# Layer 0 of a four-layer convolution stack: depthwise taps as one product per 4x4 patch, joined with pixels on partitions

## The chip, the cores and the metric

The kernel runs on one core of a Trainium2 chip. A core has five engines with a queue of their own each: TensorE (matrix products, with a separate row for its weight loads in the profile, PE and PEld), VectorE (DVE), ScalarE (ACT), GpSimd (POOL) and SyncE (SP, used for issuing transfers). Products land in PSUM, eight banks of 2 KB per partition; everything else lives in SBUF (128 partitions) or in device memory. The metric is the device time of one execution in microseconds, as the median of three runs: 3287.07 us (3285.98 to 3290.96).

## The reference

The input is x, 8 images of 128 channels and 56x56 pixels, float32. Four residual layers follow each other, `x = x + layer(norm(x))`. The change touches only the first:

```python
# 7x7 windows of 8x8 pixels; 8 heads of 16 channels; 4 windows chosen per window
xw = windows of groupnorm(x)
q, k, v = split(xw @ W_qkv + b_qkv)
v_img = v put back into an image
lepe = depthwise 3x3 convolution of v_img (padding 1) + lepe_b
r_idx = top 4 of mean(q) * SCALE . mean(k) over windows
attn = softmax(q * SCALE . k of the four windows)     # per head, 64 x 256
o = attn @ (v of the four windows)
x = x + (o + lepe) @ W_o + b_o
```

Layer 1 is a recurrent layer along the pixels, layer 2 a grouped 3x3 convolution with a 1x1 part, layer 3 two 3x3 convolutions with batch norm.

## The kernel before

**Layout.** X holds all images with channels on partitions. A strip is 7 windows, 8 rows of pixels, 448 columns (`BLK`); an image has 7 strips, the layer 56. Windows are worked on in pairs: 196 pairs, 3.5 to a strip. `xw` holds the normalised image window by window.

**A pair.** `gather` (GpSimd) copies the keys of the four chosen windows into `ks` (line 498, eight copies for a pair) and makes `qm`, the queries of the window twice, once masked to the even and once to the odd heads (line 500). `scores` makes their products on four row groups at once (539). `maxima` takes row maxima on VectorE (546), four ops; `halve` splits them in two bfloat16 parts on GpSimd (552, 553), `flip` transposes these on TensorE (558), `flipped` copies them on ScalarE (562). `shifted` makes the transposed scores less the maxima (571, 581), `exponentials` runs on ScalarE (591). `values` multiplies with the chosen windows' values (605), which `fetch` brings from `vpix` in device memory into `ring` (518). `turned` transposes 32x32 blocks on VectorE so that pixels lie on partitions (617), `divide` takes the reciprocal of the sums and the quotients `ot` (626, 629), and then transposes `ot` back to channels on partitions (638) into a strip's tile `o`.

**A strip's jobs.** `normalise` (278, VectorE; three of the first image's strips on ScalarE, 276) and `sums` (283); keys (291), image (301, with `image_end` 307 into `vrow`, stored to `vimg`, the value image with a border, by `store` 202 or 204), pixels (319, stored to `vpix`), queries (390, 394). `neighbours` (407) loads three copies of a strip's rows with their upper and lower rows from `vimg`, shifted by a column each, 32 channels at a time, from GpSimd's queue. `depthwise` (420) makes the taps: for each of three rows and four channel groups a product with 96 rows (3 shifts x 32 channels) and 448 columns, summed in PSUM over the three rows; ScalarE adds the bias (427). `join` adds `o` to it (438, GpSimd; the last one on VectorE). `project` multiplies with W_o (446) and adds to X in one VectorE op (451); the result is kept in `xkeep` (452) and measured for layer 1 (460).

**Order.** The order on TensorE, ScalarE, VectorE and GpSimd is written out by hand. Step p runs the list `SHORT` or `LONGER` of acts: scores and maxima of pair p + 2, shifted scores and exponentials of p + 1, values, turn and division of p, gathers for p + 3. A planner puts jobs with a ready and a due time into two places of each step, `one` and `two`, and small ones into `light`; the taps are `LONG` and take `two`. VectorE work such as normalisations and statistics is hooked behind the acts of a step by weights. `ahead` issues the transfers collected in `later` from GpSimd. Each act has its PSUM bank: values share a bank with the first quarter of the scores, `one` and `two` share banks with the shifted scores, swapped in `LONGER`.

Of the kernel before, what the change touches and what calls it, by code (L numbers as in the profile page):

```python
# [20 lines left out]
P = 128  # L21
# [13 lines left out]
PW = HW + 2  # L35
EPS = 1e-5
# [10 lines left out]
def conv_stack_kernel(ctx: ExitStack, tc: tile.TileContext, a: dict, out: bass.AP):  # L47
# [81 lines left out]
    with ExitStack() as l0:  # L129
# [18 lines left out]
        wlep = load("wlep", [3 * CL, 3, 4, CL], a["lepe_d"], nc.sync)  # L148
# [4 lines left out]
        lbv = c0.tile([P, 1], F32, name="lbv")  # L153
        ones = c0.tile([P, P], BF16, name="ones")
# [13 lines left out]
        vimg = [dram.tile([P, PW, PW], F32, name=f"vimg{i}", tag=f"vimg{i}") for i in range(2)]  # L168
        vpix = [dram.tile([NWIN + 1, WPX, P], F32, name=f"vpix{i}", tag=f"vpix{i}") for i in range(B)]
        vrow = []  # L170
        for i in range(2):
            t = c0.tile([P, WS, PW], F32, name=f"vrow{i}", tag=f"vrow{i}")
            if i == 0:
                nc.gpsimd.memset(t, 0.0)
                for k in range(2):
                    nc.sync.dma_start(vimg[k][:, 0:PW:PW - 1, :], t[:, 0:2, :])
            else:
                nc.gpsimd.memset(t[:, :, 0:PW:PW - 1], 0.0)
            vrow.append(t)
# [3 lines left out]
        qs, ks, selrs, v3s, lepes, os_, st1, norms = {}, {}, {}, {}, {}, {}, {}, {}  # L183
# [77 lines left out]
        def preparation(b):  # L261
# [9 lines left out]
            def normalise(i, scalar=False):  # L271

                dst = xw[:, i * NW : (i + 1) * NW, :].rearrange("p j (u v) -> p j u v", v=WS)
                src = X[:, b, i * BLK : (i + 1) * BLK].rearrange("p (u j v) -> p j u v", u=WS, v=WS)
                if scalar:
                    nc.scalar.activation(dst, src, AF.Identity, bias=st["off"], scale=st["r"])
                else:
                    nc.vector.tensor_scalar(dst, src, st["gm"], st["r"], ALU.subtract, ALU.mult)
# [20 lines left out]
            def image_mm(i):  # L299
                st["pv", i] = psum([P, BLK], f"pvt_{b}_{i}")  # L300
                nc.tensor.matmul(  # L301
                    st["pv", i], wqkv[:, 2 * P :], xwf[:, i * BLK : (i + 1) * BLK], start=True, stop=True
                )

            def image_end(i):
                t = vrow[(b * NBLK + i) % 2]
                nc.scalar.activation(
                    t[:, :, 1 : 1 + HW].rearrange("p u (j v) -> p j u v", v=WS),
                    st["pv", i].rearrange("p (j u v) -> p j u v", u=WS, v=WS),
                    AF.Identity, bias=bqkv[:, 2:3],  # L310
                )
                store(begun, nc.sync, vimg[b % 2][:, 1 + i * WS : 1 + (i + 1) * WS, :], t)
# [72 lines left out]
        def queries(b, i):  # L385
            st = {}

            def mm():
                st["pq"] = psum([P, BLK], f"pq_{b}_{i}")
                nc.tensor.matmul(st["pq"], wqkv[:, :P], xwf[:, i * BLK : (i + 1) * BLK], start=True, stop=True)  # L390

            def end():
                q = strip.tile([P, NW, WPX], F32, name=f"q_{b}_{i}", tag="q", bufs=2)
                nc.scalar.activation(
                    q.rearrange("p j x -> p (j x)"), st["pq"], AF.Identity, bias=bqs, scale=QSCALE
                )
                qs[b, i] = q

            return fill(mm, end)

        def neighbours(b, i):

            t = strip.tile([3 * CL, 4, (WS + 2) * PW], F32, name=f"v3_{b}_{i}", tag="v3", bufs=1)
            flat = vimg[b % 2].rearrange("(g c) u v -> c g (u v)", c=CL)
            for k in range(3):
                n = (WS + 2) * PW - k
                nc.gpsimd.dma_start(
                    t[k * CL : (k + 1) * CL, :, :n], flat[:, :, i * WS * PW + k : i * WS * PW + k + n]
                )
            v3s[b, i] = t  # L410

        def depthwise(b, i):
            st = {}

            def mm():
                rows = v3s.pop((b, i)).rearrange("p g (u v) -> p g u v", v=PW)
                st["pl"] = psum([P, WS, HW], f"plep_{b}_{i}")
                for dy in range(3):
                    for g in range(4):
                        nc.tensor.matmul(  # L420
                            st["pl"][g * CL : (g + 1) * CL], wlep[:, dy, g, :], rows[:, g, dy : dy + WS, :HW],
                            start=(dy == 0), stop=(dy == 2),
                        )

            def end():
                lepes[b, i] = strip.tile([P, WS, HW], F32, name=f"lep_{b}_{i}", tag="lep")
                nc.scalar.activation(lepes[b, i], st["pl"], AF.Identity, bias=lbv)
# [5 lines left out]
        def join(b, i):  # L433

            o, t = os_.pop((b, i)), lepes[b, i]
            engine = nc.vector if (b, i) == (B - 1, NBLK - 1) else nc.gpsimd
            t = t.rearrange("p u (j v) -> p u j v", v=WS)
            engine.tensor_add(t, t, o.rearrange("p j (u v) -> p u j v", v=WS))

        def project(b, i):  # L440
# [3 lines left out]
            def mm():  # L444
                st["py"] = psum([P, BLK], f"py_{b}_{i}")
                nc.tensor.matmul(  # L446
# [1501 lines left out]
```

## Time and profile before

| | |
|---|---|
| Median of three runs | 3287.07 us |
| Profiled execution, its own time | 3289.69 us |
| Span of it in the trace | 3287.8 us |
| TensorE busy, whole span | 3188.8 us (97%) |
| VectorE busy | 2306.0 us (70%) |
| ScalarE busy | 1271.0 us (39%) |
| GpSimd busy | 1486.4 us (45%) |
| First and last turn of quotients (`turned`, 196 of them) | 52.3 and 1168.3 us |
| GpSimd `qm`, 392 of them | 393 ns each |
| GpSimd `lep` addition, 55 of them | 1.13 us each |
| ScalarE tap end, 56 of them | 0.64 us each |

Lines of the profile's groups read: line of the code, engine, operation, tile written and tiles read, shapes, count, then the busy time in us and the mean of one in ns, then the time that the engine idled before them and what ended it. A float32 product appears as two records. Products are pipelined, so the duration of one contains its way through the array; the chain of waits shows what each adds. The granted TensorE clock was 0.99 of full speed on the mean.

### The profile page before, as it was taken

The page shows a single profiled execution, that of the slowest core. Times are in us where ns is not written, and L with a number is a line of the kernel's source. Part 1 is how long each engine was busy: PE and PEld are TensorE (multiplying, and loading weights), DVE is VectorE, ACT ScalarE, POOL GpSimd, SP SyncE. Part 2 cuts the span into 40 slices and gives each one's busy share as a digit, 9 for nine tenths or more (in the row PEclk, how much of TensorE's full clock was granted, in tenths as well). Part 3 has the DMA queues.
Part 4 walks back from the last instruction along what each step waited for, and adds up shares of the span by engine and source line. Part 5 has one row for each costly group of instructions (what it writes and reads, how often), then busy time and mean ns, then how long its engine had stood idle before and what let it go on. Part 6 is the DMA issues. An engine that isn't in the chain of part 4 may idle for free.

```text
span 3287.8 us, 104432 instructions
## 1 busy us (share of the span) xinstructions
PE 3188.8 (97%) x40780; PEld 2690.5 (82%) x40780; DVE 2306.0 (70%) x5747; ACT 1271.0 (39%) x2423; POOL 1486.4 (45%) x4147
## 2 busy tenths in 40 slices
PE   7999999999999989999999999999999999899998
PEld 5767677676776679999999999999999943498998
DVE  5888888788887866665555555555523257799999
ACT  4555555555555522222111111111122244455654
POOL 5787887878787833332222222222100066322221
PEclk8999999999999999999999999999999999999999
DMA  5455555555455411110000000000022156300001
GB/s 155 133 142 133 142 138 134 143 131 142 121 139 148 117 55 49 49 49 22 1 1 1 1 1 1 1 1 1 23 61 61 50 154 165 81 25 35 30 30 41
DMA packets 188167, 239.09 MB, mean 73 GB/s; under 512 B 42848, under 2 KB 137568, under 8 KB 187664
## 3 DMA queue, kind: packets, MB, share of 16 engines
q0 software_dynamic: 40896, 123.47, 13.8%
q1 hardware_dynamic: 130256, 101.95, 10.7%
q10 hardware_dynamic: 16512, 6.90, 0.9%
q8 instruction: 324, 5.31, 0.7%
q14 instruction: 179, 1.47, 0.1%
HBM read 133.64 MB, written 67.56 MB: 61 GB/s over the span
## 4 chain that ended last, share of the span: by engine, by line
PE 78%; DVE 15%; issue 2%; POOL 2%; ACT 1%; DMA 1%; ACTq 0%; POOLq 0%; SPq 0%; DVEq 0%
PE ps L1086 27%; PE q L1051 9%; PE s L539 6%; PE po L605 6%; PE po L1116 5%; PE t L581 4%; PE plep L420 4%; PE pc L1327 4%; PE pi L1021 3%; DVE nmax L546 2%; PE t L571 2%; PE py L446 1%; PE pc L1335 1%; PE pvp L319 1%; PE pvt L301 1%
## 5 line engine op out<-in xcount | busy, mean ns | idle before, releaser
L1086 PE MATMUL ps<-hs,w_gates 128*128 128x136 f32 x7680 | 928.8, 279 | 0.0
L1086 PEld LDWEIGHTS ps<-hs,w_gates 128*128 128x128 f32 x7680 | 911.6, 190 | 4.5
L1100 ACT ACTIVATE hs<-v 128x272 f32<-128x272 f32 x538 | 212.4, 405 | 1167.2 <-DVE v L1098 1167.2
L546 DVE TENSOR_REDUCE nmax<-s 128x2 f32<-128x512 f32 x784 | 486.6, 685 | 166.9 <-PE s L539 165.1
L1098 DVE TENSOR_TENSOR v<-ps,g 128x272 f32<-128x272 f32 x538 | 216.5, 411 | 493.8 <-PE ps L1086 406.6
L591 ACT ACTIVATE e<-t 128x512 f32<-128x512 f32 x784 | 429.7, 596 | 341.2 <-PE t L581 263.1
L1039 POOL TENSOR_TENSOR d<-inp 128x136 f32<-128x136 f32 x186 | 87.8, 472 | 788.9 <-DVE inp L1027 788.9
L498 POOL COPY ks<-kT 128x64 f32 x1568 | 297.2, 235 | 122.8 <-PE t L581 65.5
L605 PE MATMUL po<-e,ring 128*32 128x64 f32 x12544 | 244.9, 230 | 6.9 <-DVE nmax L546 5.7
L605 PEld LDWEIGHTS po<-e,ring 128*32 128x32 f32 x12544 | 217.9, 149 | 31.9 <-DVE nmax L546 8.4
L581 PE MATMUL t<-qm,ks 32*128 32x128 f32 x6272 | 237.8, 273 | 1.5 <-issue 1.5
L539 PE MATMUL s<-ks,qm 32*128 32x256 f32 x3136 | 234.0, 403 | 4.3 <-ACT vp L342 2.1
L581 PEld LDWEIGHTS t<-qm,ks 32*128 32x128 f32 x6272 | 220.6, 187 | 3.6 <-issue 2.3
L1573 PE MATMUL pc3b<-vb,u_w2c_t 128*128 128x196 f32 x1152 | 203.9, 340 | 19.7 <-DVE vb L1554 19.7
L1573 PEld LDWEIGHTS pc3b<-vb,u_w2c_t 128*128 128x128 f32 x1152 | 200.3, 197 | 22.0 <-DVE vb L1554 21.8
L1573 PE MATMUL pc3a<-va,u_w1c_t 128*128 128x196 f32 x1152 | 197.2, 331 | 7.4 <-DVE d_pc3a L1590 3.3
L1116 PE MATMUL po<-hs,xw 128*128 128x272 f32 x744 | 204.0, 397 | 0.2
L1573 PEld LDWEIGHTS pc3a<-va,u_w1c_t 128*128 128x128 f32 x1152 | 192.8, 191 | 10.9 <-issue 8.7
L539 PEld LDWEIGHTS s<-ks,qm 32*128 32x128 f32 x3136 | 146.5, 185 | 34.5 <-DVE logit L364 4.0
L1051 PE MATMUL q<-d,mixed 128*128 128x136 f32 x1116 | 160.2, 279 | 0.5 <-DVE g L1065 0.3
L500 POOL TENSOR_TENSOR qm<-q,hmask 128x128 f32<-128x128 f32 x392 | 154.0, 393 | 0.0
L1116 PEld LDWEIGHTS po<-hs,xw 128*128 128x128 f32 x744 | 132.0, 190 | 22.2 <-ACT hs L1100 0.6
(304 smaller groups left out, 5417.0 us busy)
## 6 DMA issues: line engine op xcount, KB each, us to landing
ring<-vpix SPq DMA_DIRECT2D x1176, 32.0 KB
v<-vimg POOLq DMA_DIRECT2D x56, 290.0 KB, 3.9
v<-vimg POOLq DMA_DIRECT2D x56, 289.5 KB, 4.7
v<-vimg POOLq DMA_DIRECT2D x56, 289.0 KB, 5.6
kept<-g SPq DMA_DIRECT2D x56, 272.0 KB, 2.4
g<-kept SPq DMA_DIRECT2D x56, 272.0 KB, 2.6
xkeep<-X POOLq DMA_DIRECT2D x56, 224.0 KB, 2.6
vimg<-vrow POOLq DMA_DIRECT2D x54, 232.0 KB, 2.5
```

Of the source, the lines that this page charges most:

```text
L498: nc.gpsimd.tensor_copy(kw[:, t : t + 1, :], ks[b][:, bass.ds(at, 1), :])
L539: nc.tensor.matmul(s_["s"][g][:, o, :], w["qm"][h].rearrange("p h x -> p (h x)"), w["kw"][h], start=True, stop=True,)
L546: nc.vector.tensor_reduce(s_["nmax"][:, :, g], s_["s"][g], AX.X, ALU.max, negate=True)
L581: nc.tensor.matmul(s_["t"][g][:, o, c], w["kw"][h, c * P : (c + 1) * P], w["qm"][h].rearrange("p h x -> p (h x)"), start=False, stop=(o == ...
L591: nc.scalar.activation(s_["e"][g], s_["t"][g], AF.Exp)
L605: mm = nc.tensor.matmul(po[g * CL : (g + 1) * CL, h, o], flat[:, at : at + 8 * CL - 7 : 8], s_["e"][g][:, o, c, h * WPX : (h + 1) * WPX], ...
L1051: nc.tensor.matmul(q[n // 3][:, n % 3], w, x, start=True, stop=True)
L1086: nc.tensor.matmul(ps[f][:, i], whh[:, k, m * P : (m + 1) * P], prev[k // 2][:, (s - 1) % 2, k % 2].rearrange("p c b -> p (c b)"), start=( ...
L1098: nc.vector.tensor_tensor(v[:, i : i + n], ps[f][:, i : i + n], x, ALU.add)
L1100: nc.scalar.activation(to, x, AF.Tanh)
L1116: nc.tensor.matmul(po, wout[:, k, :], hs[k // 2][:, :, k % 2], start=(k == 0), stop=(k == KH - 1))
L1573: nc.tensor.matmul(bank[:, half].rearrange("p (y x) -> p y x", x=H4), u[:, dy, k, :], v[:, k, i * RB + dy : i * RB + dy + RB, :], start=(d ...
```

## The change

Five parts belong together.

1. The value image is stored in four planes, by the parity of row and column, each 29x29 with its border, and with channels in another order (`first`), which the new weight `wvi` and bias `bvi` bring about. So that a plane's values come in one piece, windows in `xw` hold their pixels by parity too: `normalise` writes four parts in four ops. The image product reads `xw` in runs of four. `image_end` writes `vrow` as four stretches of 116 values, stored by two transfers.
2. `neighbours` loads, with four transfers, four copies of four plane rows for each of 16 groups of 8 channels: a partition holds one of the 16 positions of a 4x4 patch (four planes by four shifts) of one of 8 channels. `depthwise` then makes one product for each group: 128 rows, 32 outputs (4 pixels of a 2x2 block by 8 channels), 112 columns, nothing to sum over. VectorE transposes the result from PSUM (and clears one window's columns), so that pixels lie on partitions.
3. `divide` keeps `ot`; `join` adds the taps to it pair by pair on GpSimd, two steps later, and `back` transposes the sum to channels on partitions on VectorE. The bias of the taps goes through W_o once (`offset`) into `bo2`.
4. `project` reads runs of four and adds to X in four ops, one for each parity.
5. `qm` and its GpSimd op go: ScalarE writes the queries twice with masked scales and biases (`qscale`, `qbias`).

The planner's due times and the lists of acts follow: taps one step earlier, beside them the first ready job in `one` always, projection ready a step later, queries due later.

```diff
             def normalise(i, scalar=False):
-                dst = xw[:, i * NW : (i + 1) * NW, :].rearrange("p j (u v) -> p j u v", v=WS)
-                src = X[:, b, i * BLK : (i + 1) * BLK].rearrange("p (u j v) -> p j u v", u=WS, v=WS)
...
+                dst = xw[:, i * NW : (i + 1) * NW, :].rearrange("p j (a c u v) -> p a c u j v", a=2, c=2, u=4)
+                src = X[:, b, i * BLK : (i + 1) * BLK].rearrange("p (u a j v c) -> p a c u j v", u=4, a=2, v=4, c=2)
+                for k in itertools.product(range(2), range(2)):
+                    to, x = dst[:, k[0], k[1]], src[:, k[0], k[1]]
...
+                        nc.vector.tensor_scalar(to, x, st["gm"], st["r"], ALU.subtract, ALU.mult)
...
             def image_mm(i):
+                st["pv", i] = psum([P, 4 * WS // 2, NW, WS // 2], f"pvt_{b}_{i}")
+                x = xw[:, i * NW : (i + 1) * NW, :].rearrange("p j (s v) -> p s j v", v=WS // 2)
+                nc.tensor.matmul(st["pv", i], wvi, x, start=True, stop=True)
             def image_end(i):
...
-                store(begun, nc.sync, vimg[b % 2][:, 1 + i * WS : 1 + (i + 1) * WS, :], t)
+                for up in range(2):
+                    at = (i * WS // 2 + up) * HP
+                    store(
+                        begun, nc.sync,
+                        vimg[b % 2][2 * up : 2 * up + 2, :, at : at + SPAN].rearrange("l c x -> c l x"),
+                        t[:, up * (2 * SPAN + 2) : up * (2 * SPAN + 2) + 2 * SPAN].rearrange("p (l x) -> p l x", l=2),
+                    )
...
+                q = qs[b, i] = strip.tile([P, NW, 2, WPX], F32, name=f"q_{b}_{i}", tag="q", bufs=2)
+                for h in range(2):
+                    nc.scalar.activation(
+                        q[:, :, h], st["pq"].rearrange("p (j x) -> p j x", x=WPX), AF.Identity,
+                        bias=qbias[:, h : h + 1], scale=qscale[:, h : h + 1],
+                    )
...
         def neighbours(b, i):
+            t = strip.tile([P, MID, SPAN], F32, name=f"v3_{b}_{i}", tag="v3", bufs=1)
+            flat = vimg[b % 2].rearrange("l (c g) x -> (l c) g x", g=MID)
+            for k in range(4):
+                at = (i * WS // 2 + k // 2) * HP + k % 2
+                n = min(SPAN, HP * HP - at)
+                nc.gpsimd.dma_start(t[k * CL : (k + 1) * CL, :, :n], flat[:, :, at : at + n])
...
         def depthwise(b, i):
...
+                for m in range(4):
+                    for g in range(4):
+                        n = 4 * g + m
+                        patch = bass.AP(t.tensor, t.offset + n * SPAN, [part, [4, NW], [HP, 4], [1, 4]])
+                        nc.tensor.matmul(
+                            pl[g * CL : (g + 1) * CL, m, odd : odd + NW], wlep[:, n, :], patch, start=True, stop=True,
+                        )
             def end():
-                nc.scalar.activation(lepes[b, i], st["pl"], AF.Identity, bias=lbv)
+                nc.vector.memset(st["pl"][:, :, (1 - odd) * NW], 0.0)
+                t = lepes[b * NBLK + i] = strip.tile([P, 4, 4, CL], F32, name=f"lep_{b}_{i}", tag="lep")
+                nc.vector.transpose(
+                    t.rearrange("p m n r -> p (m n r)"), st["pl"].rearrange("p m j u v -> p (m j u v)")
                 )
...
+        def join(p):
+            to = pairs[p]["ot"].rearrange("p k h (q c) -> p k (h q) c", c=FEW)
+            for s in sorted({2 * p // NW, (2 * p + 1) // NW}):
+                x = lepes[s][:, :, p - s * NW // 2].rearrange("p m (k c) -> p k m c", c=FEW)
+                nc.gpsimd.tensor_tensor(to, to, x, ALU.add)
+        def back(p):
+            to = outs[:, 2 * p % OUTS : 2 * p % OUTS + 2].rearrange("p o (k x) -> p k o x", k=4)
+            nc.vector.transpose(to, pairs.pop(p)["ot"].rearrange("p k h c -> p k (h c)"))
...
-                nc.vector.scalar_tensor_tensor(X[:, b, cols], st["py"], bo, X[:, b, cols], ALU.add, ALU.add)
+                x = X[:, b, cols].rearrange("p (u a x c) -> p a c u x", u=4, a=2, c=2)
+                for k in itertools.product(range(2), range(2)):
+                    to, y = x[:, k[0], k[1]], st["py"][:, k[0], k[1]]
+                    nc.vector.scalar_tensor_tensor(to, y, bo2, to, ALU.add, ALU.add)
...
-                qm = win.tile([P, 2, WPX], F32, name=f"qm_{W}", tag="qm", bufs=5)
-                nc.gpsimd.tensor_tensor(
-                    qm, qs[b, i][:, j : j + 1, :].broadcast_to((P, 2, WPX)),
-                    hmask.rearrange("p (h o) -> p h o", o=1).broadcast_to((P, 2, WPX)), ALU.mult,
-                )
...
-                    job(max(q - 7, -1), q - 5 + (i < 4 and not b), lambda b=b, i=i: queries(b, i))
-                job(q + 2, q + 2, lambda b=b, i=i: depthwise(b, i), True, LONG)
-                job(last + 2, last + 5, lambda b=b, i=i: project(b, i), name=("project", b, i))
+                    job(max(pair_of(b, i * NW - NW - 1) - 1, -1), q - 3, lambda b=b, i=i: queries(b, i))
+                job(q + 1, q + 1, lambda b=b, i=i: depthwise(b, i), True, LONG)
+                job(last + 3, last + 5, lambda b=b, i=i: project(b, i), name=("project", b, i))
...
-                one, two = one if len(ready) > (MANY if p > 20 else 8) else None, long
+                two = long
...
-        SHORT = """fetch0 scores shifted gather max0 max1 values exp0 max2 exp1 max3 halve ahead one light two flip exp2
-            root turned divide end1 exp3 flipped lit hooks tails end2 fetch1"""
-        LONGER = """fetch0 scores shifted gather max0 max1 values exp0 max2 exp1 max3 halve ahead two exp2 root turned
-            divide flip light one exp3 flipped lit hooks tails end2 end1 fetch1"""
+        SHORT = """fetch0 scores shifted gather join max0 max1 values exp0 max2 exp1 max3 halve ahead one light two flip exp2
+            root back turned divide end1 exp3 flipped lit hooks tails end2 fetch1"""
+        LONGER = """fetch0 scores shifted gather join max0 max1 values exp0 max2 exp1 max3 halve ahead two exp2 root back
+            turned divide end2 flip light one exp3 flipped lit hooks tails end1 fetch1"""
```

## The prediction

> **What bounds the kernel now.** All edits lie in layer 0, the first 1172 us of the span; the later layers stay as they are. I read the stretches first, then the waits, then the chain, then the rows of the operations that change. The stretches (one line of them), with the busy time of each engine in 200 us:
>
> ```profile
> core 0: us, PE busy (x) PEld busy (x) DVE busy (x) ACT busy (x) POOL busy (x), PEclk, DMA share, GB/s
> ...
> 500.00:700.00 200.00, 195.77 (x4421) 140.43 (x4421) 167.97 (x359) 113.04 (x221) 161.86 (x526) 0.99 0.51 135
> ```
>
> TensorE is never free, VectorE (84%) and GpSimd (81%) follow closely, ScalarE (57%) has room. The waits between 100 and 1100 us (total, times, longest) say who is ahead:
>
> ```profile
> DVE nmax L546 <- PE s L539: 131.9, 129, 3.8
> ...
> DVE turned L617 <- PE po L605: 8.5, 25, 1.5
> ```
>
> VectorE waits for the scores of most pairs, so TensorE sets the pace. The chain (start, us, what) gives the real cost of TensorE's pieces, which durations of pipelined products do not:
>
> ```profile
> 586.38 1.70 PE pk L291 x4
> 588.08 0.11 PE flip L558 x2
> 588.19 1.08 PE s L539 x16
> 589.27 0.45 PE t L571 x3
> 589.72 0.90 PE t L581 x31
> 590.63 1.18 PE po L605 x63
> 591.80 2.26 PE plep L420 x24
> 594.06 0.22 PE flip L558 x2
> ...
> 597.79 0.95 PE pk L291 x2
> 598.74 0.75 PE pvt L301 x2
> ```
>
> A pair of windows costs TensorE 1.08 + 0.38 + 0.89 + 1.17 + 0.11 = 3.63 us, and each job put beside it 0.75 to 0.96, the taps 2.26. The first and last turn of the quotients start at 52.27 and 1168.35 us: 195 steps of 5.72 us.
>
> **TensorE.** A strip (56 of them, 3.5 pairs each) had 12 tap products of 448 columns on four column groups, 24 records. It gets 16 of 112 columns, 32 records. By columns that is 2.26 x 32 x 112 / (24 x 448) = 0.75 us. By the product with the values (64 records of 64 columns, 128x32 weights, 1.17 us) it is 0.59 if each record costs the same and 1.02 if columns count. I take 0.85, so 1.41 us less per strip, 79 us in all if nothing took its place. The other products keep their columns. That the moving operand comes in runs of four values (patches, image, output projection) has no row; bounds are nothing and the old 2.26.
>
> **VectorE.** The rows (count | busy us, mean ns):
>
> ```profile
> L1122 DVE SCALAR_TENSOR_TENSOR X<-po,vecs,X 128x136 f32<-128x136 f32 x160 | 65.7, 457 | 37.5 <-PE po L1116 37.5
> ...
> L278 DVE TENSOR_SCALAR xw<-X,gm,r 128x448 f32<-128x448 f32 x53 | 37.1, 701 | 0.0
> L451 DVE SCALAR_TENSOR_TENSOR X<-py,bo,X 128x448 f32<-128x448 f32 x56 | 36.3, 648 | 2.4 <-PE py L446 2.4
> ...
> L1122 DVE SCALAR_TENSOR_TENSOR X<-po,vecs,X 128x128 f32<-128x128 f32 x26 | 10.3, 443 | 6.2 <-PE po L1116 6.2
> ...
> L1298 DVE TENSOR_SCALAR pad<-X,gm_l,r_l 128x952 f32<-128x952 f32 x7 | 8.8, 1264 | 0.3
> ...
> L1298 DVE TENSOR_SCALAR pad<-X,gm_l,r_l 128x896 f32<-128x896 f32 x9 | 6.6, 738 | 0.0
> ```
>
> - Residual update: one of 448 becomes four of 112 that touch every second value of X. From 648 = 448 x 1.04 + 180 an op of 112 costs 0.30; from line 1122, whose X elements are all apart (slope (457 - 443)/8 = 1.75 ns, rest 0.22), 0.415. Four: 1.2 to 1.66 us; I take 1.5, nearer the row with separate elements. Added 0.85.
> - Normalisation: likewise four of 112. 0.23 fixed (701 less 448 x 1.04) and 1.04 to 1.75 ns per value give 0.35 to 0.43; line 1298 does its 896 at twice the rate of its 952, with 0.27 fixed, which gives 0.33. Four: 1.3 to 1.75; I take 1.5. Added 0.8.
> - Tap end: ScalarE's 0.64 goes, VectorE gets a transpose of 128x512 from PSUM, 0.45 + 256 x 1.04 ns = 0.72 from the turn of 128x256, and a clear of 64 columns between 0.06 (the smallest clear) and 0.2. Together 0.85.
> - The transposes of `ot` (0.31 a pair) become `back` (0.31): nothing.
>
> The division gains. Its median is 0.29 us, its longest 1.28:
>
> ```profile
> L629 DVE TENSOR_TENSOR ot<-turned,rden x196: 291/292/1284, 53.0 to 1169.1; 128x128 f32<-128x128 f32 x196
> ```
>
> At 604.03 GpSimd's `lep` addition (1.13) starts, and the division of 604.10 takes 1.21: two-input ops of the two engines seem to exclude each other. The mean of 478 ns means (0.478 - 0.292) x 196 = 36 us of VectorE. That addition goes; the new join of 128 columns (0.39, from `qm`'s row) stands beside the maxima, which read PSUM.
>
> Per pair VectorE was busy 4.7 us: maxima 2.49, turn 0.45, reciprocal 0.20, division 0.29, transpose 0.31, some 0.1 between dependent ones = 3.85, and its hooks. These grow by (0.85 + 0.8 + 0.85)/3.5 = 0.71.
>
> [...] No row here has a step of two.
>
> **The plan.** A step lasts about as long as the greater of TensorE's work in it and VectorE's from one turn to the next, since the scores need the bank that the previous turn frees and the hooks stand behind that turn. Before, steps with taps cost TensorE 3.63 + 2.26 = 5.89 and others 5.3 to 5.5; VectorE stayed below. Following the planner's rules with the new due times, pairs 98 to 104 become (TensorE; VectorE hooked in the step before; greater):
> - 98 keys, image 5.23; update 5.35; 5.35
> - 99 taps 4.48; sums 4.44; 4.48
> - 100 projection, queries 5.51; tap end, two statistics (0.6 each) 5.90; 5.90
> - 101 pixels, keys 5.44; update and normalisation 6.85; 6.85
> - 102 taps 4.48; sums, statistics 5.04; 5.04
> - 103 queries, image 5.31; tap end, two statistics 5.90; 5.90
> - 104 projection, pixels 5.54; normalisation 5.35; 5.54
>
> That is 39.06/7 = 5.58 against 38.82/7 = 5.55 by the same rule before. Over all 196 pairs it gives 5.58 against 5.515, +0.066, because the thirteen small variance ops (2.3 us) also land on steps that VectorE now ends: +13 us. With four ops at 1.2 us in both groups it is 5.456 (-12), at 1.75 and 1.66 5.677 (+32). The trace has 5.72, so 0.21 above its sum. I keep this excess: the division's collisions go, but two engines that alternate as the bound leave less slack.
>
> **GpSimd.** `qm` goes (7 x 0.39 = 2.75 a strip), `lep` too (1.13); 4 joins (one pair in seven touches two strips) come at 0.39 = 1.6. Issues:
>
> ```profile
> L407 POOL DMA_DIRECT2D v<-vimg x168: 550/558/626, 41.1 to 1157.7; - x168
> ...
> L202 POOL DMA_DIRECT2D vpix<-vp x49: 563/771/818, 96.4 to 1016.8; - x49
> ```
>
> The first writes 128 runs, the second 512. Neighbours become four of 512 runs (464 B): 4 x 0.77 - 3 x 0.57 = +1.4; the image store two of 256, about 0.64 each, +0.7. Sum -0.2 of some 16 us a strip. But the step after each taps now holds copies 1.5, join 0.4, halves 0.44, ring 0.54 and 3.1 of issues, 6.0 us, and `halve` and `join` of the next pair queue behind them: TensorE's flip and VectorE's `back`, then the turn, wait for these. If all were exposed it is 1.4 x 56 = 77 us, if hidden nothing; these steps last 5.9 or more, so I take 10. Transfers land in 3.8 to 6 us and have three steps; DMA is busy half the time. SP gets one more issue in each of two early image stores, lying behind 2 us of other work.
>
> **ScalarE** trades the tap end (0.64) for a second half of the queries (0.64): nothing, while its idle 43% remains; without it 0.64 x 56 = 36.
>
> **Ends.** The start is a VectorE chain (12.4 to 18.8 us: four normalisations, seven sums): 4 x 0.8 + 0.3 for two small scalings = +3.5. The last projection waits one step longer, for join and `back`: about +1. Two more weight loads on ScalarE's queue (0.45 us to issue each), two more border stores on SP's and a longer clear of `vrow` on GpSimd (+0.4) lie ahead of the first normalisation, while ScalarE idles 8 us and SP is between loads: nothing; without that cover about 1.
>
> Sum: 13 + 10 + 3.5 + 1 = +27.5. The profiled execution took 3289.69 us (span 3287.8 and 1.9 around it), 2.6 above the median of 3287.07; on that median 3314.6, so 3315.
>
> **The rivals.** *The cuts are cheap and the taps' gain shows.* Place: the eight ops of 112. At 0.25 us each, the rule of the greater gives 5.385, -25 us; with 2.5 for the ends and GpSimd hidden, 3264. It decides below about 0.30 each, where the gain of 12 equals GpSimd's 10 and part of the ends. For it: TensorE really loses 79 us and line 1298 doubles its rate on even rows. Against it: the fixed part of both rows.
>
> *GpSimd takes the bound.* If half of the 77 us shows, +39 in place of +10: 3344. For it: POOL is already 81% busy, and TensorE waited on `halves` in places. Against: steps after taps are long anyway.
>
> *The taps do not get cheaper*, since runs of four or 32 weight loads keep them at 2.26: tap steps return to 5.89 instead of about 4.9, +1 x 56: 3371. Against: the quotients' products with 128x32 weights at 18 ns a record.
>
> **How the numbers follow.** Forecast 0.50 (own range 3293 to 3337, from the lower and upper op prices), cheap cuts 0.30, GpSimd 0.14, taps not cheaper 0.06. The range leaves out most of the last and the far tails: 3262 to 3362. No change means within 0.2% (6.6 us, about what can be told); it takes 0.05 of the cheap cuts and 0.03 of the forecast. So faster 0.25, same 0.08, slower 0.67.
>
> **What would show it.** Right: taps about 0.85 us on the chain with steps of 4.5 to 5.0, VectorE busy above 90% between 100 and 1100 us, its waits for scores well under 132 us, the chain full of maxima and split ops, longest division below 0.7. Wrong: ops of 112 at 0.25 or less; GpSimd named as the one that `back` or the flip waits for; taps still above 2 us.

## The result, and the profile after

The changed kernel takes 3303.92 us (median; 3294.16 to 3306.33), the kernel before 3290.28 us beside it: a ratio of 1.0039, 95% interval 1.0026 to 1.0051. It is 0.39% slower, 13 us. The profiled execution took 3306.33 us, the longest of its eight, and its span is 3304.5 us; the profile before had 3289.69 and 3287.8.

Where the 16.7 us of span lie can be read from the starts of the turns of the quotients. First to last turn took 1116.1 us before and 1121.2 us after (195 steps of 5.723 and 5.750 us): +5.1. The first turn starts at 58.86 us and no longer at 52.27: +6.6. From the last turn to layer 1's first product of statistics it is 7.5 us and no longer 5.6: +1.9. The other 3 us lie in the later layers, which the change doesn't touch.

So the steps are hardly longer, but TensorE's saving is gone. The stretches of the changed kernel (busy us of each engine, clock, DMA):

```profile
core 0: us, PE busy (x) PEld busy (x) DVE busy (x) ACT busy (x) POOL busy (x), PEclk, DMA share, GB/s
...
500.00:700.00 200.00, 188.64 (x4614) 143.72 (x4606) 172.89 (x437) 115.95 (x225) 164.44 (x516) 1.00 0.62 142
```

In this stretch TensorE is busy for 7 us less than before and now stands still 11 us in 200; no other engine has become full. VectorE stands at 86%, GpSimd at 82%. The chain of the whole span says the same; the page of the kernel before, then that after:

```profile
PE 78%; DVE 15%; issue 2%; POOL 2%; ACT 1%; DMA 1%; ACTq 0%; POOLq 0%; SPq 0%; DVEq 0%
```

```profile
PE 67%; DVE 18%; POOL 5%; issue 5%; ACT 2%; DMA 2%; ACTq 1%; POOLq 1%; DVEq 0%; SPq 0%
```

TensorE lost 11 points of the chain. VectorE and GpSimd took 3 each, 3 went to "issue", which is time for which the profile names no cause, and ScalarE, the engines' queues and the transfers have the rest. The taps alone stood on the chain with 125 us in 54 of the 56 strips before, and stand there with 28 us in 29 strips now. The waits between 100 and 1100 us:

```profile
DVE outs L471 <- POOL ot L465: 68.0, 81, 2.6
...
DVE nmax L577 <- PE s L570: 49.2, 63, 1.5
...
PEld L589 <- POOL halves L584: 32.1, 90, 2.0
```

VectorE's wait of the maxima for scores fell from 131.9 to 49.2 us. In its place VectorE waits 68 us for the join (`back`, line 471, behind GpSimd's addition of line 465), and TensorE's flip waits 32 us for GpSimd's halves, for which it had waited 15 us in the kernel before:

```profile
PEld L558 <- POOL halves L553: 15.2, 34, 2.2
```

The chain between 560 and 640 us:

```profile
564.57 0.97 DVE X L487 x4
566.24 1.00 DVE xw L292 x4
567.24 2.40 DVE nmax L577 x4
...
576.63 0.72 DVE lep L451
577.35 0.50 DVE xm L297
577.85 0.54 DVE st L496
578.38 2.39 DVE nmax L577 x4
581.68 1.89 POOL v L429 x3
583.67 0.54 POOL v L429
...
598.91 1.11 PE plep L443 x29
...
622.37 0.88 ACT q L415 x2
```

The reader sees every engine on it: the split operations of VectorE (four take 0.97 and 1.00 us), the tap end and the statistics ahead of the maxima, GpSimd's issues of the neighbours, the taps (1.11 us here, about 0.9 in most strips, 2.26 before), and ScalarE's two halves of the queries. The rows of the changed work (count | busy us, mean ns):

```profile
L429 POOL DMA_DIRECT2D v<-vimg x224 | 147.6, 665 | 13.7 <-issue 13.3
...
L465 POOL TENSOR_TENSOR ot<-ot,lep 128x128 f32<-128x128 f32 x224 | 101.6, 454 | 6.3 <-DVE ot L660 2.8 <-DVE lep L451 1.4
...
L415 ACT ACTIVATE q<-pq,qbias,qscale 128x448 f32<-128x448 f32 x112 | 75.2, 724 | 9.4 <-PE pq L410 8.5 <-DVE sel L390 0.6
...
L292 DVE TENSOR_SCALAR xw<-X,gm,r 128x112 f32<-128x112 f32 x212 | 59.1, 359 | 0.0
L487 DVE SCALAR_TENSOR_TENSOR X<-py,bo,X 128x112 f32<-128x112 f32 x224 | 58.9, 325 | 1.5 <-PE py L481 1.5
...
L451 DVE STREAM_TRANSPOSE lep<-plep 128x512 f32<-128x512 f32 x56 | 40.1, 717 | 2.2 <-DVE plep L449 0.4
```

By the starts of the turns, the step in which the taps start lasts 5.42 us on average (5.69 before) and the one behind it, into which they run, 5.66 (5.91). The one before these lasts 5.98 (5.64) and the one behind them 6.18 (5.56). The two steps with taps became shorter and their neighbours longer.

### The profile page after: what moved, and what is told of

It reads as the page before. It is cut to its first block, busy times and chain, and to the rows that moved or that the text cites. A ratio compares the mean times of both kernels' runs of the same rounds, so it can differ in the third digit from the quotient of the medians.

```text
span 3304.5 us, 105617 instructions
## 1 busy us (share of the span) xinstructions
PE 3143.1 (95%) x41230; PEld 2707.2 (82%) x41230; DVE 2327.2 (70%) x6160; ACT 1280.1 (39%) x2432; POOL 1482.2 (45%) x4034
## 4 chain that ended last, share of the span: by engine, by line
PE 67%; DVE 18%; POOL 5%; issue 5%; ACT 2%; DMA 2%; ACTq 1%; POOLq 1%; DVEq 0%; SPq 0%
PE ps L1112 27%; PE q L1077 9%; PE po L1142 5%; PE po L636 5%; PE t L612 3%; PE pc L1353 3%; PE s L570 3%; PE pi L1047 3%; DVE nmax L577 2%; POOL ks L534 1%; PE pc3b L1599 1%; PE t L602 1%; PE pc L1361 1%; PE pvp L339 1%; DVE u_pc3b L1718 1%
## 5 line engine op out<-in xcount | busy, mean ns | idle before, releaser
L636 PEld LDWEIGHTS po<-e,ring 128*32 128x32 f32 x12544 | 220.8, 149 | 51.6 <-DVE nmax L577 19.3
L570 PE MATMUL s<-ks,q 32*128 32x256 f32 x3136 | 240.4, 409 | 10.0 <-ACT vp L362 6.1
L612 PE MATMUL t<-q,ks 32*128 32x128 f32 x6272 | 242.0, 275 | 6.4 <-issue 6.4
L612 PEld LDWEIGHTS t<-q,ks 32*128 32x128 f32 x6272 | 223.7, 190 | 11.9 <-issue 8.6
L570 PEld LDWEIGHTS s<-ks,q 32*128 32x128 f32 x3136 | 149.9, 188 | 45.5 <-issue 7.6
L429 POOL DMA_DIRECT2D v<-vimg x224 | 147.6, 665 | 13.7 <-issue 13.3
```

Source lines behind the costliest of these rows:

```text
L570: nc.tensor.matmul(s_["s"][g][:, o, :], w["qm"][h].rearrange("p h x -> p (h x)"), w["kw"][h], start=True, stop=True,)
L612: nc.tensor.matmul(s_["t"][g][:, o, c], w["kw"][h, c * P : (c + 1) * P], w["qm"][h].rearrange("p h x -> p (h x)"), start=False, stop=(o == ...
L636: mm = nc.tensor.matmul(po[g * CL : (g + 1) * CL, h, :, o], flat[:, at : at + 8 * CL - 7 : 8], s_["e"][g][:, o, c, h * WPX : (h + 1) * WPX ...
```

## The experiments

Each was timed beside the kernel before, which had medians of 3289.0 to 3290.4 us. Versions are compared by their ratios to it; a difference of 0.001 in a ratio is 3.3 us. From the intervals, two ratios can be told apart from about 0.0015 on, 5 us.

**The join first.** On GpSimd the join goes ahead of the gather's eight copies of the same step.

```diff
-SHORT = """fetch0 scores shifted gather join max0 ...
+SHORT = """fetch0 scores shifted join gather max0 ...
-LONGER = """fetch0 scores shifted gather join max0 ...
+LONGER = """fetch0 scores shifted join gather max0 ...
```

> On GpSimd the join of a pair now stands ahead of the gathers of its step, so it waits for nothing of that step. Theory G (the gain went into VectorE waiting for GpSimd: back for join, 68 us between 100 and 1100 us): that wait falls under 15 us, the step of 5.75 us goes to about 5.6, and the time falls by 20 to 40 us against the changed kernel, below the kernel before. Theory V (the eight ops of 112 fill VectorE, as the prediction has it): the wait turns into other VectorE work, the time stays within 6 us of the changed kernel.

Measured: 3291.15 us, ratio 1.0008 (0.9999 to 1.0017), 10 us faster than the changed kernel. The first waits of its list:

```profile
ACT e L622 <- PE t L612: 242.1, 161, 2.9
ACT e L622 <- PE po L636: 81.8, 138, 2.8
DVE nmax L577 <- PE s L570: 80.5, 93, 1.5
POOL halves L583 <- DVE nmax L577: 79.3, 97, 2.4
```

The wait for the join fell to 4.2 us, and the maxima wait for scores for 80 us and no longer 49. So 68 us of listed wait were worth 10 us of time; most of the rest became other waits. The gain lies between what the two theories expected.

**The transposes back later.** On VectorE `back` goes behind the turn of the same step.

```diff
-            root back turned divide end1 ...
+            root turned back divide end1 ...
```

> The transpose back of pair p - 2 stands behind the turn of pair p instead of ahead of it, so the scores' bank is free before VectorE waits for the join. Theory G: half of the wait of 68 us is now hidden behind 0.42 us of turn and does not hold TensorE; 8 to 20 us faster than the changed kernel. Theory V: within 6 us of it, since VectorE does the same work in another order.

Measured: 3292.21 us, ratio 1.0006 (0.9997 to 1.0015), 11 us faster. The wait for the join is 19.3 us here. The other end of the same dependence, with the same gain.

**The cuts undone.** The residual update and the normalisation are one operation of 448 again; this kernel leaves out that the products then expect the pixels in another order.

```diff
-for k in itertools.product(range(2), range(2)):
-    to, y = x[:, k[0], k[1]], st["py"][:, k[0], k[1]]
-    nc.vector.scalar_tensor_tensor(to, y, bo2, to, ALU.add, ALU.add)
+nc.vector.scalar_tensor_tensor(X[:, b, cols], st["py"]..., bo2, X[:, b, cols], ALU.add, ALU.add)
```

> The residual update and the normalisation are one op of 448 each again (pixels then stand in another order than the image product and the projection assume, so the values are not those of the reference; all other work is as in the changed kernel). VectorE loses 1.05 + 1.12 - 0.65 - 0.70 = 0.82 us a strip, 46 us in all. Theory V: 25 to 45 us faster than the changed kernel. Theory G: the step stays bound by the order of join and back, 0 to 15 us faster, most of it at the start (about 2 us) and in steps that hold both ops.

Measured: 3289.99 us, ratio 1.0003 (0.9993 to 1.0012), 12 us faster. VectorE's two rows fall from 104 to 68 us in 1000, some 40 us over layer 0, so that about a third of it was on the path. With no cut at all the kernel is just as fast as before: the cuts alone don't explain why the taps' gain is missing. The wait for the join rises to 82.5 us.

**The loads of the third image on another queue.** Its first two go out on SyncE's queue. They were meant to stand behind the stores of the first image; in the trace they go out at 15.33 and 15.72 us, well ahead of all of these stores.

```diff
-load_x(b, i, i + 1, nc.gpsimd)
+load_x(b, i, i + 1, nc.sync if b == 2 and i < 2 else nc.gpsimd)
```

> The first two loads of the third image go through SP's queue, behind the stores of the first image's values, instead of GpSimd's. Theory S (the start lost 6.7 us, of which 5.5 because GpSimd, freed of the mask op, issues these loads 2 us earlier, into the stores that ScalarE's last copy waits for): the first turn comes at 53 to 55 us instead of 58.9 and the time falls by 4 to 6 us. Theories G and V, which place the whole loss in the steps: no change of the first turn beyond 1 us.

Measured: 3295.76 us, ratio 1.0024 (1.0014 to 1.0034), 5 us faster, at the limit of what can be told; the chain shows it clearly. The changed kernel's, and then this one's:

```profile
29.36 5.74 DMA vpix<-vp
35.20 0.27 ACT vp L362
35.46 0.14 issue
35.60 2.10 PE s L570 x16
```

```profile
29.53 3.10 DMA vpix<-vp
32.73 0.27 ACT vp L362
33.13 2.10 PE s L570 x16
```

The store that frees the buffer of `vp` takes 5.74 us in the changed kernel and 3.10 us with the loads issued some 14 us before it; in the kernel before it took 2.22. GpSimd issues the loads at 28.41 us in the changed kernel, 0.95 us in front of this store (29.36); before, they came at 30.56, 3.1 us behind it (27.45). The first turn comes 2.3 us earlier here, at 56.59 us and not by 55 as expected.

**The masks back on GpSimd.** ScalarE writes the queries once, and GpSimd masks them in each gather as before.

```diff
-for h in range(2):
-    nc.scalar.activation(q[:, :, h], ..., bias=qbias[:, h : h + 1], scale=qscale[:, h : h + 1])
+nc.scalar.activation(q, st["pq"], AF.Identity, bias=bqs, scale=QSCALE)
...
+nc.gpsimd.tensor_tensor(qm, qs[b, i][:, j : j + 1, :]..., hmask..., ALU.mult)
```

> The changed kernel with the queries written once by ScalarE (one activation a strip instead of two) and masked by GpSimd in each gather again, so 7 products of 0.39 us a strip (2.75 us, 154 us over layer 0) go back to GpSimd and 0.72 us a strip (40 us) leave ScalarE; the queries are due at the old times. Theory that ScalarE's second half of the queries costs nothing, since ScalarE is 57% busy, and that GpSimd's room is what the change lives on: 20 to 60 us slower than the changed kernel, 3325 to 3365 us, with the wait of the quotients' divided values for the join well above its 68 us. Theory that the second half lies on the path (the values products wait 8.5 us, 19 times, for the queries; the chain shows 0.88 us of it): up to 15 us faster than the changed kernel where GpSimd's part stays hidden, 3289 to 3300 us. Start: X loads of GpSimd go behind the first masks again, so the first turn comes some 1 to 2 us earlier than 58.9 us by either.

Measured: 3370.79 us, ratio 1.0238 (1.0223 to 1.0252), 65 us slower than the changed kernel, a little more than the first theory's 20 to 60. Its waits:

```profile
DVE outs L469 <- POOL ot L463: 153.6, 121, 3.3
PEld L592 <- POOL halves L587: 115.3, 130, 2.8
ACT nm L596 <- PE flip L592: 111.0, 122, 3.4
PE flip L592 <- POOL halves L587: 64.7, 74, 2.4
```

GpSimd holds up VectorE's `back` (154 us) and TensorE's flip (115 us in the row of its weight loads, 65 in that of its products). GpSimd has 154 us more to do here and ScalarE's relief is in the same figure, so GpSimd's time is on the path by 65/154 or more, if the queries' old due times, which came back with the masks, cost nothing; that was not tested. The change's joins and issues are only affordable because the masks left. The start did not get better, as had been expected: the loads go out at 29.13 us, still in front of the store at 29.36, which takes 5.61 us, and the first turn is at 59.42.

**The masked queries alone.** In the kernel before, only the queries change. In this kernel the queries of 43 of the 56 strips are computed after the normalisation that overwrites their input with the next image's values; number and shape of the instructions are those of the computation.

```diff
+for h in range(2):
+    nc.scalar.activation(q[:, :, h], ..., bias=qbias[:, h : h + 1], scale=qscale[:, h : h + 1])
-nc.gpsimd.tensor_tensor(qm, qs[b, i][:, j : j + 1, :]..., hmask..., ALU.mult)
...
-job(max(q - 7, -1), q - 5 + (i < 4 and not b), lambda b=b, i=i: queries(b, i))
+job(max(pair_of(b, i * NW - NW - 1) - 1, -1), q - 4, lambda b=b, i=i: queries(b, i))
```

> The kernel before with one part of the change alone: ScalarE writes the queries of a strip twice, masked, and GpSimd no longer masks them in each gather; taps, residual and normalisation stay as before. GpSimd loses 2.75 us a strip (154 us of busy time), ScalarE gains 0.72 us a strip (40 us). Theory that TensorE sets the pace there and ScalarE's part is free: within 8 us of before, 3281 to 3297 us, the waits of the maxima for scores still near 132 us. Theory that ScalarE's second half is on the path: 10 to 36 us slower, 3299 to 3325 us, with waits of TensorE for the queries and for the values' copies in the list. Theory that GpSimd's load held before back through its gathers and collisions: 5 to 25 us faster, 3264 to 3284 us. The start should show the loads of X going out about 2 us earlier on GpSimd's queue, in front of the first image's stores, and so a first turn later by 1 to 5 us by each of them.

Measured: 3309.38 us, ratio 1.0064 (1.005 to 1.0077), 21 us slower than before, though GpSimd's busy time fell from 801 to 668 us in 1000. In the kernel before, GpSimd's relief is worth nothing that shows, and ScalarE's second half (or the later place of the job) costs. The start gives a cross-check of the loads: without masks they go out at 29.34 us, but the store stands ahead of them at 27.68 and takes 2.35 us. So it is the order of loads and store that counts, and in the changed kernel the store itself stands 1.9 us later.

**The queries twice.** To take the place of the job out of it: in the kernel before, the activation of the queries is made twice with the same values, and nothing else changes.

```diff
+for again in range(2):
     nc.scalar.activation(q.rearrange("p j x -> p (j x)"), st["pq"], AF.Identity, bias=bqs, scale=QSCALE)
```

> The kernel before with ScalarE's activation of the queries made twice (the same values written again), 0.64 us more for each of the 56 strips, 36 us of ScalarE in all, and nothing else changed. Theory of the prediction, that ScalarE's idle 43% hides it: within 4 us of before, 3285 to 3294 us. Theory that the evacuation stands between a product and the next step's copies of the maxima and bank, on the path: 15 to 36 us slower, 3304 to 3326 us.

Measured: 3311.46 us, ratio 1.0068 (1.0054 to 1.0082), 22 us slower than before, of 36 us that ScalarE has more to do; its idle share is 41%. The chain between 580 and 640 us:

```profile
617.99 0.75 PE pq L390 x2
619.31 0.54 ACT q L395
619.88 0.63 ACT q L395
...
622.83 0.60 ACT e L592
623.48 2.46 PE plep L421 x24
```

Both activations stand one after the other between a product of TensorE and the next. An idle share of 41% hides none of them at that place.

**The taps twice.** In the changed kernel every patch product is made twice.

```diff
+for again in range(2):
     nc.tensor.matmul(pl[g * CL : (g + 1) * CL, m, odd : odd + NW], wlep[:, n, :], patch, start=True, stop=True)
```

> The changed kernel with every patch product of the taps made twice (the second overwrites the first with the same values), so TensorE has 32 more records a strip at the rate of the 0.85 to 0.94 us that the chain shows for 28 to 32 of them: 48 to 53 us more of TensorE's work over the 56 strips, on the steps with taps, and nothing more for any other engine. Theory that TensorE is no longer what ends the steps with taps (VectorE, GpSimd and their waits do): less than 15 us slower than the changed kernel, 3304 to 3319 us. Theory that TensorE still ends them, so that the saving of the taps was real but was given back elsewhere: 40 to 53 us slower, 3344 to 3357 us.

Measured: 3342.98 us, ratio 1.0166 (1.0152 to 1.018), 42 us slower than the changed kernel. The chain (taps alone) between 580 and 640 us:

```profile
588.89 1.86 PE plep L444 x64
...
613.70 2.36 PE plep L444 x62
...
632.05 1.92 PE plep L444 x64
```

64 records take 1.86 us where 29 or 30 took 0.88, so TensorE got about 0.97 x 56 = 54 us more, and three quarters of it show. My theory that TensorE no longer ends these steps is wrong: added work is on the path, though the taps stand on the chain in only half of the strips before they are doubled. Read the other way round, with taps of 1.86 us, not far from the old 2.26, the other parts of the change make the kernel 53 us slower than before, and halving the taps gives 42 us back. So the cheaper taps were a real saving, which the other parts of the change used up. The taps alone, without the other parts, were not run.

**The three small moves together.** Join first, `back` later, loads on SyncE's queue; the diffs are those above.

> The three small moves together that were measured singly: the join ahead of the gather on GpSimd (alone -12.8 us against the changed kernel), VectorE's transposes back behind the next turn (-11.7), and the first two loads of the third image on the queue of SyncE (-8.1). Theory that they take away different waits: the sum, -32 us, 3272 us, faster than before. Theory that the first two take away the same wait (the divided values' wait for the join, 68 us in all): about -21 us, 3283 us. Theory that each only uncovers the next limit (TensorE's own work and VectorE's maxima): -13 to -15 us, 3289 to 3291 us, no better than the best single one.

Measured: 3291.21 us, ratio 1.0002 (0.9993 to 1.0011), 12 us faster than the changed kernel and no better than the best of the three alone. The last of the three theories holds: what is cleared away at one place is a wait for the next.

**The planner told of the new costs.** On top of the three moves the planner, which spreads VectorE's jobs over the steps by weights, gets weights for what they now cost; the old ones gave the tap end none.

```diff
-weight[p] += 7
+weight[p] += 10
...
-fixed.append((at[i], 7, lambda b=b, i=i: once(preparation, b)[6](i)))
+fixed.append((at[i], 11, lambda b=b, i=i: once(preparation, b)[6](i)))
...
+for b, i in itertools.product(range(B), range(NBLK)):
+    weight[placed["taps", b, i]] += 9
```

> The kernel with the three moves, and the planner told of the new costs: the projection weighs 10 instead of 7 (its residual update is four operations), the normalisation 11 instead of 7, and the tap end, which weighed nothing, 9. So jobs with much work of VectorE are put on different steps. Theory that steps on which several of these pile up (one of 8.1 us in the changed kernel) carry what is left: 5 to 15 us faster than the three moves alone, with no step above 7.5 us. Theory that VectorE is not the bound and its placement hidden: within 4 us of the three moves alone.

Measured: 3282.18 us, ratio 0.9974 (0.9965 to 0.9983): 9 us faster than the three moves alone, 21 us faster than the changed kernel, and 0.26% faster than the kernel before, the only version here that is. Mean step 5.627 us. The limit of 7.5 us for a single step wasn't met: the longest is 8.98 us (9.03 in the changed kernel). The step before the taps' start, the one in which they start and the two behind it now last 5.93, 5.73, 5.00 and 6.09 us, against 5.98, 5.80, 5.29 and 6.00 with the three moves alone; the gain is mainly in the step into which the taps run. The two profiled executions lie 20 us apart and the medians 9, so the steps show where the gain lies better than how large it is. Which of the three weights brings it was not tested by itself.

**Half of the queries by VectorE.** On top of that, VectorE writes the second half of each strip's queries.

```diff
+if h:
+    nc.vector.tensor_scalar(to, x, by, c, ALU.mult, ALU.add)
+else:
+    nc.scalar.activation(to, x, AF.Identity, bias=c, scale=by)
```

> The kernel with the three small moves and the planner told of the new costs (3282.2 us), and the second half of each strip's queries written by VectorE in place of ScalarE: 0.72 us a strip (41 us) leave ScalarE, about 0.7 us a strip (40 us) go to VectorE, beside each other rather than one after the other. Theory that the two halves one after the other are on the path (0.88 to 0.93 us of ScalarE on the chain at every strip): 5 to 20 us faster than without this move, 3262 to 3277 us. Theory that VectorE (85% busy) is as near the bound: within 4 us or up to 20 us slower, 3278 to 3302 us.

Measured: 3294.97 us, ratio 1.0014 (1.0005 to 1.0023), 13 us slower than without it, as the second theory had it. Three of its waits:

```profile
PEld L604 <- DVE q L418: 37.8, 24, 3.9
...
PE t L604 <- DVE q L418: 28.6, 27, 3.5
DVE q L418 <- ACT q L420: 15.1, 28, 0.9
```

TensorE's copies of the maxima need the bank that the queries leave, and now wait up to 3.9 us for VectorE, whose half stands behind its turn and divisions in 28 of the 56 strips and behind a normalisation in most others. The half is not dear (0.74 us), but it stands in a queue that is late.

**The neighbours on SyncE's queue.** The planner's version again (3282.18 us), with four loads a strip issued elsewhere.

```diff
-nc.gpsimd.dma_start(t[k * CL : (k + 1) * CL, :, :n], flat[:, :, at : at + n])
+nc.sync.dma_start(t[k * CL : (k + 1) * CL, :, :n], flat[:, :, at : at + n])
```

> The kernel with the three small moves and the planner told of the new costs (3282.2 us), with the four loads of a strip's neighbours issued from SyncE's queue and no longer from GpSimd's: 4 x 0.666 us a strip, 149 us of GpSimd's 815 us per 1000, leave GpSimd, of which nothing else changes. Theory that GpSimd's work is on the path about as the masks were that went back to it (154 us cost some 66 us and more): 30 to 80 us faster than without the move, 3202 to 3252 us. Theory that GpSimd's issues stand beside other engines' work (it waits 69 us for the maxima and 34 us for the shifted products): 0 to 10 us faster, 3272 to 3282 us. Theory that SyncE's queue, which waits in order for each section of the ring to come free (141 us behind the quotients' products), brings the ring's rows or the neighbours late: slower than without the move, above 3285 us, with waits of TensorE on the transfers of the ring or the neighbours in the list.

Measured: 3365.98 us, ratio 1.0234 (1.022 to 1.0248), 86 us slower than without it. From its waits and from its chain:

```profile
DVE plep L449 <- PE plep L443: 58.8, 19, 6.3
...
PE plep L443 <- DMA v<-vimg: 52.8, 17, 5.5
PEld plep L443 <- issue: 51.1, 13, 5.7
```

```profile
574.72 0.62 SPq L429
575.39 0.62 SPq L429
576.05 6.72 DMA v<-vimg
582.91 1.72 PE plep L443 x32
```

The last of these four issues is out 6.9 us ahead of the taps, and the taps wait for its transfer. Over all strips the last issue is out 8.9 us ahead (median; least 4.7), and the wait for it is part of that; without the move it is 10.5 us (least 6.6). The step in which the taps start lasts 7.10 us instead of 5.73. In the records of the version without the move SyncE's instructions already fill 777 of the 1000 us, 603 of them 1062 issues of the ring's rows (0.57 us on average) and much of the rest the loading of their addresses (in the changed kernel 91 such loads of 0.98 us in the median), none of which the page counts as busy; the four loads had to stand behind those.

## Why the prediction was right, and where its steps were not

The time (3303.9 against 3315, range 3262 to 3362) and the sign held, but the change is half the forecast, 13 us for 27.5, and a range from 25 us faster to 75 us slower says little of the mechanism. The steps:

- **Taps (TensorE): right.** 0.85 us was predicted; the chain shows 0.88 to 1.11. "79 us in all if nothing took its place" was right to keep its condition: the taps made twice show that three quarters of added work arrive.
- **Residual update and normalisation (VectorE): mis-sized.** Predicted 1.5 us each for four operations, from fixed costs of 0.18 and 0.23 us. The chain has 0.97 and 1.00 us, 0.25 for each. An operation lasts 0.325 to 0.36 us in the rows, but the next begins before it ends; my rows were of operations that stand alone. Both cuts together add 0.62 us a strip to the chain's pieces (0.97 + 1.00 for 0.65 + 0.70), where my sum had 1.65. What of the 0.25 us is fixed can only be estimated, since no run has operations on every second value in a second size. The normalisations of line 1298 in the kernel before take 1264 ns for 952 values and 1609 ns for 1288, so 1.03 ns a value, near the 1.04 of the prediction; by that rate 0.13 us of the 0.25 would be fixed, less than either of my two figures. The maxima of the changed kernel, 512 values each (read from PSUM), start 0.60 us apart, which by the same rate would leave 0.07 us.
- **The rival of cheap cuts had its condition, not its result.** It named 0.25 us for an operation, 0.30 as the point that decides, and 3264 us. The operations cost 0.25, and the time is 3304. So the step that failed is the rule behind both sums, "a step lasts about as long as the greater of TensorE's work in it and VectorE's". Steps lengthen by a part of whatever any engine gets: 42 of 54 us more for TensorE, 22 of 36 for ScalarE (in the kernel before), 12 of 40 less for VectorE, about 65 of 154 for GpSimd, though in the changed kernel none of the engines is full (TensorE is busy for 93% of the time between 100 and 1100 us, VectorE for 85%). Within a step scores, maxima, halves, flip, copies, exponentials, quotients, turn follow each other through four engines.
- **Tap end and division: right.** Transpose 0.717 and clear 0.112 us; the divisions' longest is 0.391 us (1.284 before), their mean 293 ns.
- **GpSimd: mechanism right, durations and place off.** Neighbours 0.665 us each (0.77 predicted), image stores 0.733 (0.64), joins 0.454 (0.39). "`halve` and `join` of the next pair queue behind them" is what happened: 68 us of waits at `back`, 32 at the flip (15 before). I took 10 us; putting the join first, or `back` later, gives back 10 to 11 us. That the two figures agree is partly luck: the 10 was chosen between nothing and 77.
- **ScalarE at "nothing, while its idle 43% remains": wrong.** The idle share remained and the second half still cost: in the kernel before it is 22 us. The predicted bound without cover, 36, was nearer. In the changed kernel this part was not measured by itself.
- **The start: mechanism right, one missing.** +3.5 was predicted, +6.6 measured. The split operations hold up TensorE's first key-side products by 1.4 us (20.40 against 18.98). What I had not seen: GpSimd's loads now go out in front of the first image's last store, since they come 2.2 us earlier and the store 1.9 us later, and the store takes longer; issued earlier on SyncE's queue, they give 2.3 us back. The masks' leaving alone is not the reason, as the two runs on the masks show. The other 2.9 us were not traced to a part. The tail took 1.9 us for a predicted 1.
- **What would show it: mixed.** Taps about 0.85 and divisions below 0.7 came; waits for scores "well under 132" too (49.2), though not since VectorE is full: it was to be above 90% busy and is at 85%. Steps with taps were to last 4.5 to 5.0 us and last 5.42 and 5.66. The chain holds maxima and split operations, but 67% of it is still TensorE's over the whole span. Of the three signs of being wrong two came: operations at 0.25, and GpSimd named as the one that `back` and the flip wait for.

The forecast's +27.5 therefore got its sign and came within 11 us partly by luck, for partly wrong reasons: VectorE's cuts were taken too high, ScalarE and the start too low, and the rule of the greater, which by 0.25 us an operation would have given -25, doesn't describe a step. The single effects don't add up (join, `back` and loads: 10, 11 and 5 us alone, 12 together), so no sum of them can be closed to the 13 us; which share each part has in the changed kernel stays open.

## What to carry to other kernels

When the work of a step passes through several engines one after the other, no engine's idle share is cover: ask where in that ring the added instruction stands, and price it at a part of its duration (0.3 to 0.8 in the four cases here) unless it can be moved out of the ring. A move to a less busy engine counts only after looking at its queue's order, and at queues whose issues the page doesn't count as busy. And where a planner places work by costs, a change of the costs belongs to the change: here the planner's weights, the order of two queues and the place of two loads turned 0.39% slower into 0.26% faster.

## What the runs showed of the hardware

- Four operations of VectorE of 128x112 in a row (lines 487 and 292 of the changed kernel) follow each other every 0.24 to 0.25 us although each takes 0.325 or 0.36.
- The last store of the first image that the chain shows at 2.22 us in the kernel before takes 5.74 us when two loads of 224 KB were issued from another engine 0.95 us before it, 5.61 when they were issued 0.23 us before it, and 3.10 when they were issued some 14 us before it.
- Between 100 and 1100 us the granted clock of TensorE was 1.00 in the planner's version, where TensorE was busy for 942 us, and 0.97 with the masks back on GpSimd, where it was busy for 898 us. Which of the two brings the other isn't shown.

```profile
100.00:1100.00 1000.00, 942.15 (x23341) 720.82 (x23340) 852.23 (x2192) 586.19 (x1133) 815.24 (x2591) 1.00 0.61 143
```

```profile
100.00:1100.00 1000.00, 898.32 (x21370) 680.56 (x21366) 798.76 (x2039) 513.55 (x1001) 870.89 (x2709) 0.97 0.56 132
```
